# Two attention fills reordered: keys ahead of the norm, a projection that catches up inside the first groups, and later queries computed inside the second fill

## The chip, the cores and the metric

The kernel runs on one core of a Trainium2 chip. The metric is the time of one execution on the device in microseconds; the median of several runs is compared. Beside the timed runs one execution was recorded by the hardware profiler; its trace gives every instruction's start and duration on the five engines: TensorE (PE, with its weight loads as PEld), VectorE (DVE), ScalarE (ACT), GpSimd (POOL) and SyncE (SP, which here only issues transfers).

## The reference, cut to what matters

A residual stream `x` of 128 rows by 256 passes through six blocks; each starts with a norm of `x`. A context of 12544 rows by 192 is read by two of them. Only these two are touched.

```python
# block 1: 16 heads of 16, keys and values from the context
q = (layernorm(x) @ Wq + bq);  k = ctx @ Wk + bk;  v = ctx @ Wv + bv
out = softmax(q k^T / 4) v            # per head, over 12544 keys
x = x + relu(out @ W1 + b1) @ W2 + b2
# block 2: causal self-attention;  block 3: mixture of 8 experts
# block 4: 16 heads of 64, keys and values from the same context
q = layernorm(x) @ Wq;  k = ctx @ Wk;  v = ctx @ Wv
x = x + softmax(q k^T / 8) v @ Wo + bo
# block 5: small attention;  block 6: two of 8 experts
```

Everything is float32. The softmax subtracts a maximum over the keys, so the scores of many keys must exist before the first exponential.

## The kernel before, in words

**First attention.** The heads are done in two octets `j` (eight heads each). For each octet the context is walked in superblocks of 1024 keys (`SB`), numbered `m`; a superblock is four groups of 256 keys, numbered `t` over everything (98 groups). One group is one turn of the loop at L545. In a turn TensorE computes `scores(t)` (L412) into two score tiles, ScalarE copies both to SBUF (`keep`, L425) and VectorE keeps a running maximum (L431, or L437 for the first range, which reads the copies). Ten groups make a range; at its end the maxima are folded (`fold`), transposed and reduced (`range_maximum`), and spread over partitions (`range_spread`). `LAG` = 13 turns later the stored scores of a group are shifted by the maximum (GpSimd and VectorE, L493), exponentiated by ScalarE (L504) and multiplied with the values (`attend`, L517). So turns 0 to 11 are a fill: scores and projections only.

The projections of keys and values are cut into four pieces per superblock: `pieces(t)` gives for g = 0 the first half of the keys, g = 1 the second, g = 2 and 3 the same for values. A unit has a part with 64 contraction rows for both halves ("tiled", L214 or L232) and a part with 128 rows per half ("whole", L217 or L239). Its two PSUM banks come from the ring `ps_w`, of which there are two in this stage; a bank is free when it has been evicted (`keys_out` L373, `values_out` L377, both on VectorE). The pieces run `AHEAD` = 4 turns ahead: pieces 0 to 3 before the loop, then piece t + 4 in turn t. Other banks are tagged "m" (maximum) and "o" (output), one each; they are empty during the first turns.

Ahead of all this stand the loads of `x` and of small tensors, the norm `ln0` with its transposes, the broadcast of the value bias (`bvb`: a matmul of one row, L132, and a copy, L342), and the queries of both octets (L348 to L356).

**Between.** After the first attention a key projection for the second attention's pass 0 (`first_keys`, advanced in steps by `fill(n)`) is slipped between the steps of the following blocks.

**Second attention.** Eight passes `j` of two heads each walk 13 superblocks, one per period `t`; `LAG` is 14 periods. In pass 0 the keys are already there or come from `fill`; each period computes scores (L933), ScalarE copies them (L950), VectorE takes the maximum (L968). After the last period of the pass the maximum is folded (L980). All eight query chunks are computed before the first period (L876 and L880).

The order of the instructions on each engine is the order in which the program writes them (`manual_schedule`). SyncE issues all transfers in program order.

Of the kernel before, what the change touches and what calls it, by code (L numbers as in the profile page):

```python
# [33 lines left out]
def perceiver(ctx: ExitStack, tc: tile.TileContext, a: dict, out: bass.AP):  # L34
# [34 lines left out]

    x = xp.tile([P, D], F32, tag="x", name="x0")  # L70
    nc.sync.dma_start(x, a["x"][0])

# [54 lines left out]
    nc.sync.dma_start(cols, a["cols"])  # L127
    nc.sync.dma_start(rows, a["rows"])
# [6 lines left out]
    def layernorm(x, name):  # L135
# [10 lines left out]
        return xn, transposed(xp, xn, 2, name + "T", tag="xnT")  # L146

    def transposed(pool, t, n, name, tag, **kw):

        tT = pool.tile([P, n, P], F32, tag=tag, name=name, **kw)  # L150
        for g in range(0, n, 4):
            m = min(4, n - g)
            pt = ps_t(f"{name}_ps{g}")
            for i in range(m):
                nc.tensor.transpose(pt[:, i * P : (i + 1) * P], t[:, (g + i) * P : (g + i + 1) * P], ident)
            nc.vector.tensor_copy(tT[:, g : g + m, :].rearrange("p c n -> p (c n)"), pt[:, : m * P])
# [34 lines left out]
    def load_context(pool, name, s, bufs):  # L191
# [6 lines left out]
        nc.sync.dma_start(lo[:, :n], a["ctxT"][0:P, k0 : k0 + n])  # L198
        for r in range(2):
            nc.sync.dma_start(  # L200
# [4 lines left out]
    def project_keys(name, wk, cx, j):  # L205

        lo, hi, h = cx
        ps = [ps_w(f"{name}_{r}") for r in range(2)]
# [12 lines left out]
    def project_values(name, wv, cx, j):  # L221

        lo, hi, h = cx
        ps = [ps_w(f"{name}_{r}") for r in range(2)]
# [79 lines left out]
    with tc.tile_pool(name="l0w", bufs=1) as lw:  # L304
        xwq = slot_weight("xwq", a["L0_xattn_Wq"])
        xwk = context_weight(lw, "xwk", a["L0_xattn_Wk"])
        xwv = context_weight(lw, "xwv", a["L0_xattn_Wv"])

        with tc.tile_pool(name="l0x", bufs=1) as work, ExitStack() as ps0:
# [20 lines left out]
            for v in vs:  # L330
                nc.gpsimd.memset(v, 1.0)
# [6 lines left out]
            _, xnT = layernorm(x, "ln0")  # L338
            pb = ps_mm("bvb_ps")
            add_row(pb[:, :D], ROW_BV, D, start=True)  # L340
            bvb = work.tile([P, D], F32, name="bvb")
            nc.vector.tensor_copy(bvb, pb[:, :D])  # L342

            qz = work.tile([P, 2, 2, P], F32, name="x0_qz")
            for j in range(2):
                pq = ps_mm(f"x0_pq{j}")
# [10 lines left out]

            def pieces(t):
# [5 lines left out]
                if g == 0:  # L364
                    ctxs[m] = load_context(work, f"x0_ctx{m}", s, 2)
# [5 lines left out]

                def keys_out(r, src):
                    nc.vector.tensor_scalar(kTs[m][:, r * h : (r + 1) * h], src[:, :h], bias, None, ALU.add)  # L373

                def values_out(r, src):
                    n = h // P
                    nc.vector.tensor_copy(  # L377
                        v[:, r * n : (r + 1) * n, 0:136].rearrange("p k (h d) -> p k h d", d=17)[:, :, :, 0:16],
                        src[:, :h].rearrange("p (k h d) -> p k h d", h=8, d=16),
                    )  # L380

                def first_half(kind, make, w, evacuate):
                    unit = make(f"x0_{kind}{m}", w, ctxs[m], j)
# [66 lines left out]
            def bank_m(name):  # L450
                return pp.tile([P, KB], F32, tag="m", name=name, bufs=1)

# [53 lines left out]
            def attend(t):  # L506
                m, g = groups[t]
                b = range_of[t]
                if first[t]:
                    os[b] = pp.tile([P, KB], F32, tag="o", name=f"x0_o{b}", bufs=1)  # L510
# [27 lines left out]
            with tc.manual_schedule():  # L538
                for t in range(AHEAD):
                    for f in pieces(t):  # L540
                        f()
# [3 lines left out]
                for t in range(len(groups) + LAG + 1):  # L545
# [22 lines left out]
                    ahead = pieces(t + AHEAD)  # L568
# [14 lines left out]
                    if ended is not None:  # L583
                        range_maximum(ended)
                    if t > LAG and last[t - LAG - 1]:
# [4 lines left out]
            with tc.manual_schedule():  # L590
# [4 lines left out]

                kw = slot("k0_wk_lo"), slot("k0_wk_hi")
# [81 lines left out]
                nc.vector.tensor_tensor(o, om, bvb, ALU.add)  # L678
# [176 lines left out]
    with tc.tile_pool(name="l1x", bufs=1) as work:  # L855
# [10 lines left out]
        with tc.manual_schedule():  # L866
# [4 lines left out]
            for g in range(2):  # L871
                pq = ps_mm(f"x1_pq{g}")
                for i in range(4):
                    j = 4 * g + i
# [411 lines left out]
```

## Time and profile before

| | |
|---|---|
| runs | 1600.96, 1606.61, 1606.82 us; median 1606.61 |
| profiled execution | 1599.54 us, span 1597.8 us |
| mean granted TensorE clock | 0.988 |
| first attention's scores (L412) start | 22.11 us |
| first exponential (L504) | 72.48 us |
| end of the first attention's output matmuls (L517) | about 470 us |
| second attention's scores (L933) start | 594.30 us |
| its first fold (L980) | 634.98 us |

The times inside the span are from the span's start. In a timeline row the columns are start, duration, engine, line, operation, output and inputs, shape and the number of instructions merged into the row. In a row of stretches they are the stretch, its length, and the busy time of PE, PEld, DVE, ACT and POOL with the number of instructions, then the granted clock, the share of the DMA engines and GB/s. The chain of waits lists what the end of a window was waiting for, step by step; "issue" in it is time in which the engine waited for nothing that the profile shows.

### The profile page before, as it was taken

To read this page: it belongs to the slowest core of one execution; us is meant where nothing else is said; L and a number is where in the kernel's file an instruction comes from. 1 tells how busy PE (TensorE), PEld (TensorE's weight loads), DVE (VectorE), ACT (ScalarE), POOL (GpSimd) and SP (SyncE) were. 2 spreads that over 40 slices of the span, in tenths; PEclk is the share of its full clock that TensorE was granted. 3 is DMA by queue.
4 is the path that set the end of the run, shared out by engine and by line. 5 is a ranking of instruction groups with operands and counts; after the bars stand their busy time and mean duration, and the time that the engine had idled before them with its cause. 6 is when DMAs were issued, how large, how long until landed. Compare 5 with 4: busy or idle time off the path is not lost.

```text
span 1597.8 us, 39754 instructions
## 1 busy us (share of the span) xinstructions
PE 1511.6 (95%) x17130; PEld 1159.9 (73%) x17130; DVE 1181.8 (74%) x1254; ACT 986.4 (62%) x1205; POOL 857.1 (54%) x554
## 2 busy tenths in 40 slices
PE   7899999999879998999999999999999999998978
PEld 4566666666545886887777777787787778787868
DVE  5898987998883327678777777777777777777952
ACT  2699888999873226665665655665565655665631
POOL 1288888888840000863863864864764764762000
PEclk9999999999999999999999999999999999999979
DMA  3111021211096760232322222222232222225930
GB/s 103 41 49 54 27 61 41 61 41 41 14 255 180 241 169 20 80 99 68 96 83 83 82 80 86 80 84 81 84 97 79 86 80 85 81 80 160 297 135 4
DMA packets 68737, 146.62 MB, mean 92 GB/s; under 512 B 8905, under 2 KB 27089, under 8 KB 68562
## 3 DMA queue, kind: packets, MB, share of 16 engines
q1 hardware_dynamic: 68562, 144.08, 30.7%
q8 instruction: 135, 2.21, 0.6%
q14 instruction: 40, 0.33, 0.1%
HBM read 143.92 MB, written 0.13 MB: 90 GB/s over the span
## 4 chain that ended last, share of the span: by engine, by line
PE 74%; DVE 13%; ACT 7%; issue 3%; DMA 1%; POOL 1%; POOLq 0%; SPq 0%; ACTq 0%; DVEq 0%
PE x_v L239 12%; PE x_s L933 11%; PE x_k L217 11%; PE x_o L1018 10%; PE x_v L232 6%; PE x_k L214 5%; PE x_s L412 5%; DVE x_mx L431 4%; ACT x_p L425 3%; PE x_o L517 2%; PE f_h L1222 2%; PE f_h L801 2%; PE f_py L818 2%; DVE x_part L1041 2%; DVE x_p L493 2%
## 5 line engine op out<-in xcount | busy, mean ns | idle before, releaser
L999 POOL TENSOR_TENSOR x_p<-x_p,x_spread 128x1024 f32<-128x1024 f32 (+1 forms) x175 | 402.7, 2326 | 161.8 <-ACT x_spread L992 161.6
L493 POOL TENSOR_TENSOR x_p<-x_p,x_spread 128x512 f32<-128x512 f32 (+1 forms) x184 | 325.6, 1824 | 127.1 <-ACT x_spread L481 67.5
L1041 DVE TENSOR_REDUCE x_part<-x_p 128x256 f32<-128x1024 f32 (+1 forms) x175 | 329.7, 1924 | 1.6 <-ACT x_p L1007 1.6
L950 ACT COPY x_p<-x_s 128x1024 f32<-128x1024 f32 (+1 forms) x200 | 197.9, 996 | 179.8 <-DVE x_mx L957 97.9
L957 DVE TENSOR_TENSOR x_mx<-x_s,x_mx 128x1024 f32<-128x1024 f32 (+1 forms) x161 | 193.4, 1201 | 127.2 <-PE x_s L933 118.7
L1046 POOL TENSOR_TENSOR x_sums<-x_sums,x_part 128x256 f32<-128x256 f32 x161 | 120.9, 751 | 306.1 <-DVE x_part L1041 305.9
L425 ACT COPY x_p<-x_s 128x1024 f32<-128x1024 f32 x196 | 193.2, 1015 | 78.8 <-PE x_s L412 64.1
L239 PEld LDWEIGHTS x_v<-ywv_lo,x_ctx_lo 128*128 128x128 f32 x1568 | 192.3, 194 | 38.3 <-issue 36.8
L1007 ACT ACTIVATE x_p<-x_p 128x1024 f32<-128x1024 f32 (+1 forms) x200 | 197.8, 1037 | 1.4 <-DVE x_p L999 1.3
L504 ACT ACTIVATE x_p<-x_p 128x1024 f32<-128x1024 f32 x196 | 196.3, 1062 | 0.2 <-DVE x_p L493 0.2
L239 PE MATMUL x_v<-ywv_lo,x_ctx_lo 128*128 128x128 f32 x1568 | 196.2, 278 | 0.0
L1018 PE MATMUL x_o<-x_p,x_v 128*64 128x128 f32 x3136 | 193.8, 276 | 0.4
L431 DVE TENSOR_TENSOR x_mx<-x_s,x_mx 128x1024 f32<-128x1024 f32 x140 | 168.0, 1220 | 31.8 <-PE x_s L412 17.2
L1018 PEld LDWEIGHTS x_o<-x_p,x_v 128*64 128x64 f32 x3136 | 169.8, 137 | 12.4 <-issue 1.7
L933 PE MATMUL x_s<-x_qT,x_kT 64*128 64x128 f32 x2744 | 178.3, 279 | 0.0
L933 PEld LDWEIGHTS x_s<-x_qT,x_kT 64*128 64x128 f32 x2744 | 160.9, 188 | 15.8 <-issue 15.4
L217 PE MATMUL x_k<-x_ctx_lo,ywk_lo 128*128 128x512 f32 (+1 forms) x364 | 171.6, 594 | 0.0
L918 ACT COPY x_v<-x_v 128x512 f32<-128x512 f32 (+1 forms) x208 | 116.1, 562 | 83.3 <-PE x_v L239 82.8
L232 PEld LDWEIGHTS x_v<-ywv_hi,x_ctx_hi 64*128 64x128 f32 x1568 | 106.1, 188 | 47.2 <-issue 24.9
L412 PE MATMUL x_s<-x_qz,x_kT 32*128 32x256 f32 x1568 | 118.6, 401 | 17.0 <-ACT x_p L425 16.8
L517 PE MATMUL x_o<-x_p,x_v 128*32 128x128 f32 x3136 | 111.8, 276 | 9.8 <-ACT x_p L504 8.9
L517 PEld LDWEIGHTS x_o<-x_p,x_v 128*32 128x32 f32 x3136 | 82.0, 109 | 53.6 <-ACT x_p L504 19.8
(252 smaller groups left out, 1764.4 us busy)
## 6 DMA issues: line engine op xcount, KB each, us to landing
x_ctx_lo<-in_ctxT_dram SPq DMA_DIRECT2D x120, 512.0 KB, 4.1
x_ctx_hi<-in_ctxT_dram SPq DMA_DIRECT2D x240, 128.0 KB, 4.0
f_w<-in_L_ffn_W_dram SPq DMA_DIRECT2D x32, 512.0 KB, 4.9
k_lo<-in_ctxT_dram SPq DMA_DIRECT2D x12, 512.0 KB, 8.3
f_gating<-n_kernel_gating_EDF_dram SPq DMA_DIRECT2D x8, 512.0 KB, 6.8
f_up<-L_ffn_kernel_up_EDF_dram SPq DMA_DIRECT2D x8, 512.0 KB, 7.0
f_wd<-ffn_kernel_down_EFD_dram SPq DMA_DIRECT2D x8, 512.0 KB, 7.7
k_hi<-in_ctxT_dram SPq DMA_DIRECT2D x24, 128.0 KB, 8.3
```

The source lines that it names most:

```text
L217: nc.tensor.matmul(ps[r][:, :h], wk[0][:, js], lo[:, r * h : (r + 1) * h], start=False, stop=True)
L232: nc.tensor.matmul(ps[r][:, ks], hi[rs, ks], wv[1][rs, js], start=(kc == 0), stop=False, skip_group_check=True,)
L239: nc.tensor.matmul(ps[r][:, kc * P : (kc + 1) * P], lo[:, r * h + kc * P : r * h + (kc + 1) * P], wv[0][:, js], start=False, stop=True, sk ...
L412: nc.tensor.matmul(st[i // 2][:, i % 2, 256 * c : 256 * c + 256], kTs[m][rs, ks], qz[rs, sbs[m][0]].rearrange("p u q -> p (u q)"), start=T ...
L425: nc.scalar.copy(ps[t][k], st[k].rearrange("p a n -> p (a n)"))
L431: nc.vector.tensor_tensor(m, st[1 - k], old, ALU.max)
L493: engine.tensor_tensor(v, v, by[:, banks].unsqueeze(2).to_broadcast([P, n, 2, 256]), ALU.add)
L517: nc.tensor.matmul(os[b][32 * i : 32 * i + 32, u * P : (u + 1) * P], v[:, 2 * g + c, 17 * (2 * i + u) : 17 * (2 * i + u) + 32], p[i // 2][ ...
L933: nc.tensor.matmul(st[:, u, c * P : (c + 1) * P], kTs[t][rs, ks], qT[rs, j, :], start=True, stop=True)
L999: engine.tensor_tensor(v, v, spreads[j].unsqueeze(2).to_broadcast([P, 2, n, P]), ALU.add)
L1018: nc.tensor.matmul(o[us, 0:P], vs[t][:, c0 + c, us], p[:, n0 : n0 + P], start=(c0 + c == 0), stop=(c0 + c == total - 1), skip_group_check= ...
L1041: nc.vector.tensor_reduce(part, v, AX.X, ALU.add)
```

## The change

In the first attention, the first superblock's context is loaded through ScalarE's queue, and the key weights move ahead of the columns and query weights on SyncE's. The first half of the first key projection comes before the norm on TensorE; the norm's transposes and the queries of octet 0 use the two halves of one score tile (`early`). Then the loop starts. Pieces 1 to 7 are done in turns 0 to 3, two per turn and one in turn 3 (`behind`); from turn 4 on it is piece t + 4 as before. The values of the first two superblocks go to the banks "m" and "o" (`spare`). Pieces below 16 (`filling`) are evicted by ScalarE, keys as an Identity activation with the bias. The queries of octet 1 come in turn 5. The value tiles are set to one only where a one is needed. The bias row's matmul moves behind the loop, and its bank is read directly by the addition; the load of `rows` moves to turn 8.

In the second attention, only query chunk 0 comes ahead of the first period; chunks 1 to 4 come in period 5 and chunks 5 to 7 in period 7, each group followed by one scaling on VectorE.

```diff
-    nc.sync.dma_start(cols, a["cols"])
-    nc.sync.dma_start(rows, a["rows"])
...
     with tc.tile_pool(name="l0w", bufs=1) as lw:
+        x = xp.tile([P, D], F32, tag="x", name="x0")
+        nc.sync.dma_start(x, a["x"][0])
+        xwk = context_weight(lw, "xwk", a["L0_xattn_Wk"])
+        nc.sync.dma_start(cols, a["cols"])
         xwq = slot_weight("xwq", a["L0_xattn_Wq"])
-        xwk = context_weight(lw, "xwk", a["L0_xattn_Wk"])
         xwv = context_weight(lw, "xwv", a["L0_xattn_Wv"])
...
-                nc.gpsimd.memset(v, 1.0)
+                nc.gpsimd.memset(v[:, :, 0:136].rearrange("p k (h d) -> p k h d", d=17)[:, :, :, 16:17], 1.0)
+                nc.gpsimd.memset(v[:, :, 136:152], 1.0)
...
+            def spare(name):
+                return bank_o(name) if name.endswith("_1") else bank_m(name)
+            def behind(t):
+                return ((1, 2), (3, 4), (5, 6), (7,))[t] if t < 4 else (t + AHEAD,)
...
-                    ctxs[m] = load_context(work, f"x0_ctx{m}", s, 2)
+                    ctxs[m] = load_context(work, f"x0_ctx{m}", s, 2, None if m else nc.scalar)
...
+                filling = t < LAG - 1 + AHEAD
                 def keys_out(r, src):
-                    nc.vector.tensor_scalar(kTs[m][:, r * h : (r + 1) * h], src[:, :h], bias, None, ALU.add)
+                    dst = kTs[m][:, r * h : (r + 1) * h]
+                    if filling:
+                        nc.scalar.activation(dst, src[:, :h], AF.Identity, bias=bias)
+                    else:
+                        nc.vector.tensor_scalar(dst, src[:, :h], bias, None, ALU.add)
                 def values_out(r, src):
...
+                    evacuated(filling, dst, src[:, :h].rearrange("p (k h d) -> p k h d", h=8, d=16))
                 def first_half(kind, make, w, evacuate):
-                    unit = make(f"x0_{kind}{m}", w, ctxs[m], j)
+                    bank = spare if kind == "v" and m < 2 else None
+                    unit = make(f"x0_{kind}{m}", w, ctxs[m], j, bank)
...
             with tc.manual_schedule():
-                for t in range(AHEAD):
-                    for f in pieces(t):
-                        f()
+                tiled, whole, k_out = pieces(0)
+                tiled()
+                whole()
+                early = ps_s("x0_early")
+                _, xnT = layernorm(x, "ln0", early[:, 0])
+                k_out()
+                queries(0, xnT, early[:, 1])
...
-                    ahead = pieces(t + AHEAD)
+                    ahead = [f for n in behind(t) for f in pieces(n)]
...
+                    if t == 5:
+                        queries(1, xnT, bank_m("x0_pq1"))
+                    elif t == 8:
+                        nc.sync.dma_start(rows, a["rows"])
...
+                pb = ps_mm("bvb_ps")
+                add_row(pb[:, :D], ROW_BV, D, start=True)
...
-                nc.vector.tensor_tensor(o, om, bvb, ALU.add)
+                nc.vector.tensor_tensor(o, om, pb[:, :D], ALU.add)
...
-            for g in range(2):
-                pq = ps_mm(f"x1_pq{g}")
-                for i in range(4):
-                    j = 4 * g + i
+            def queries(j0, j1):
+                pq = ps_mm(f"x1_pq{j0}")
+                for j in range(j0, j1):
...
+            queries(0, 1)
...
                 if t < NS:
                     fill(2 if t < 4 else 1)
+                if t in (5, 7):
+                    queries(*((1, 5) if t == 5 else (5, 8)))
```

## The prediction

> **What bounds the kernel now.** I read four views in this order: the busy shares, the busy time by stretch, the chain of waits in the first 80 us, and the timeline of the two places where the change cuts in.
>
> ```profile
> PE 1511.6 (95%) x17130; PEld 1159.9 (73%) x17130; DVE 1181.8 (74%) x1254; ACT 986.4 (62%) x1205; POOL 857.1 (54%) x554
> ```
>
> TensorE is busy 95% of the span, so a gain must come from a stretch where it stands idle or starts late. The stretches (length; then busy us of PE, PEld, DVE, ACT, POOL):
>
> ```profile
> 0.00:5.00 5.00, 0.00 (x0) 0.00 (x0) 0.72 (x4) 1.37 (x2) 4.37 (x24) 1.00 0.39 122
> 40.00:50.00 10.00, 9.14 (x85) 6.09 (x86) 7.14 (x9) 5.08 (x6) 0.00 (x0) 1.00 0.01 2
> 80.00:100.00 20.00, 19.22 (x314) 13.49 (x316) 17.64 (x21) 18.66 (x21) 20.00 (x12) 1.00 0.14 41
> ```
>
> At 80 us all engines overlap; at 40 us GpSimd has nothing to do and ScalarE is half idle: that is the fill, in which scores are stored until the first range's maximum is known. Before it, TensorE does nothing for 8 us. The start, and the chain inside the fill:
>
> ```profile
> 5.44 2.45 DVE L145 TENSOR_SCALAR ln<-x,ln_mv,ln_rstd 128x256 f32<-128x256 f32 x1
> 11.78 2.71 PE L214 MATMUL x_k<-x_ctx_hi,xwk_hi 64*128 64x512 f32 x4
> 14.42 3.78 PE L217 MATMUL x_k<-x_ctx_lo,xwk_lo 128*128 128x512 f32 x4
> 22.11 1.15 PE L412 MATMUL x_s<-x_qz,x_kT 32*128 32x256 f32 x16
> ```
> ```profile
> 43.49 0.14 DVE x_mx L437
> 43.63 0.99 issue
> 44.63 0.75 DVE x_kT L373
> 45.38 0.04 issue
> 45.42 1.16 PE x_v L232 x14
> ```
>
> The reader is to see two things. First, norm, bias row, queries, keys and values run one after another, so the first scores start at 22.11. Second, inside the fill TensorE's next projection waits for a bank that VectorE empties (L373), and VectorE gets to it only after the maxima (L437). Score groups start at 25.30, 40.12 and 54.95 for t = 1, 5, 9: 14.8 us for four groups.
>
> The second fill is another case:
>
> ```profile
> 589.11 5.26 PE L876 MATMUL x_pq<-ln3T,ywq 128*128 128x128 f32 x32
> 612.98 21.96 DVE L968 TENSOR_TENSOR x_mx<-x_p,x_mx 128x1024 f32<-128x1024 f32 x17 [0.98 <-ACT x_p L950]
> 634.98 1.89 DVE L980 TENSOR_REDUCE x_folded<-x_mx 128x256 f32<-128x1024 f32 x1
> ```
>
> All eight query chunks precede the first score (594.30), but the stage ends with the maxima: from 612.98 VectorE runs 17 of them without a hole, and the fold follows. Its queue bounds this fill, not TensorE's.
>
> **The change part by part.** Sums are against the profiled execution: 1599.5 us, span 1597.8, so 1.7 us around it. The median shown, 1606.6, is 7.1 us above it (the runs go from 1601.0 to 1606.8); I carry the difference over to the median.
>
> *Start of TensorE.* The first context block goes to ScalarE's queue at about 0.85 us instead of SP's at 6.06. In the trace its large part landed 5.8 us after issue and its small parts 4.3. By the row it would be here at about 6.3 to 6.7. The Trainium skill, "DMA: Bandwidth & Descriptors", section "Issuing engines are not separate DMA queues", speaks against a larger gain: transfers from any engine run on the same 16 engines and a second issuer saves only issue time. Up to here 1.19 MB must come in (x 128 KB, key weights 256, columns 38, context 768), against some 340 GB/s in the trace at 8 to 9.7 us: 3.5 us and about 2 us of latency, so 6.3 by that way too. x may land later than its 2.9; its norm has until 10.8. On SP's queue the query weights now wait for the context's landing (they share a completion counter) and come at about 9.5; needed at 11.9. The value weights follow at about 10 (needed at 17.8) and the second block at about 14 (needed at 23): covered, else a delay goes straight into TensorE. The columns, now behind the key weights on SP, come at about 5 and are first read at 10.9. ScalarE spends some 1.6 us on its three issues (0.5 each on SP) before its table load, which started at 3.62 in the trace: covered as well.
>
> From 6.3: key halves 2.71 (as at 11.78), one whole-key matmul 1.9 (half of 3.78), to 10.9. Two transposes 0.66, VectorE copy 0.42 with semaphores 0.1, queries of octet 0 four records 1.05, then 0.35 + 0.48 on VectorE and 0.15 of semaphores: first scores at 14.1, 8.0 us earlier. The norm (2.45 while GpSimd clears the value tiles, 0.41 for the other five in the trace) is off the path: smaller memsets are worth nothing here, but had it stayed slow it would still fit.
>
> *Catching up.* Eight groups' pieces stood ahead of, or inside, t = 0 to 3 before; now k's first half is done early and pieces 1 to 7 lie inside t = 0 to 3. TensorE pays in order: scores 1.09, k tiled 1.06, each whole half 1.07, v tiled 1.08. While the clock is low, times 1.7 (3.78 us for four L217 records at 14.4 us, 2.2 later). Here a rule and the row part. "TensorE: Matmul & The Clock Gate", section "What's actually happening", gives full clock after about 3.4 us of sustained work; in this trace matmuls start at 8.04 and the L217 records to 18.2 are still slow: 10 us. By the rule the array would be fast by 11 and the fill 2 to 3 us shorter; I take the row, slow until about 18.5.
> t0: 1.85 + 1.8 + 1.85 + 1.07, so t1 at 20.7; t1: 1.09 + 1.07 + 1.06 + 1.07 = 4.3, t2 at 25.0; likewise t3 at 29.3; t3: 2.2, t4 at about 31.4 against 35.0. Lead 3.6: more than half of the start's 8 us is given back.
>
> *Evacuation by ScalarE for t < 16.* Sixteen evictions leave VectorE (0.75 and 0.69 us). The nearest ScalarE row of this shape is L632, 0.585 us; with bias or a strided destination I take 0.6 (ends 0.4 and 1.0). Behind each wait the next group's score copies. Four groups then need: TensorE 11.1 (4.4 scores, 3.2 k, 3.3 v and 0.2), ScalarE 8 x 0.97 + 4 x 0.6 = 10.1, VectorE 8 x 1.2 = 9.6. With the holds between (a score tile cannot be overwritten before its copy of 0.97 ends) I get 12.1 per four groups against 14.8: t8 at 43.6 against 49.84, t10 at 49.5 against 57.19. Between t10 and t11, VectorE does maxima, fold and two reductions without the key and value evictions that stood between them (6.74 us before): about 5.3. t11 at 54.8 against 63.93, t12 at 58.0 to 58.4 against 67.55: 9.2 us. An eviction of 1.0 us instead of 0.6 would cost 1.3 of it. The later query pair (0.83 us on VectorE, 0.8 on TensorE at t = 5) falls into VectorE's slack, included. The instruction order has activation-table loads only where before (square root and exponential), so none is added. From t = 12 the order is the same, and the 9.2 us are carried to its end at 470.
>
> *The bias row.* Its matmul (0.69 for two records at this clock) now precedes the key fill at 471.38. The transposes of the result waited there for TensorE (end 477.3, data 477.0), so +0.65. The addition reads PSUM instead of SBUF, 0.42 either way. The late load of the rows, 5 KB, is hidden by hundreds of us.
>
> *Second fill.* Before the first score go 4 records instead of 32: 28 x 0.162 = 4.5 us less, but VectorE's 0.35 is now waited for: scores at 590.3, 4.0 earlier. VectorE would do its maxima 4.0 earlier too, until t = 5. There the maxima of t4 end at 611.6; the queued scaling waits for the sixteen records behind the scores of t5: 609.0 + 1.99 + 0.42 + 16 x 0.13 (L686, the same shape, sixteen records in 2.05) + 0.2 = 613.7. So 2.1 idle and 0.69 of scaling; at t7 0.2 and 0.55. Given back: 3.6. Net -0.4; at the 0.162 of L876 it would be +0.3, so I keep -2 and +1.5 as ends. What is moved is work into the cover of a queue that is itself the bound.
>
> Sum: -9.2 + 0.65 - 0.4 = -9.0. 1599.5 would become 1590.5; the median 1597.6.
>
> **The rivals.**
> *Early clock* (12%): the rule on the clock holds in the new order, since dense work begins at 6.3. Then -12 us, 1594.6. For it: no idle of over a microsecond in the keys. Against: 10 us in the trace.
> *The catch-up is held* (14%): ScalarE's eviction, queued behind two score copies, keeps a bank; or a context block comes late. One hold of 1 us in each of four groups: -5, 1601.6. Against: values of the first two blocks get two otherwise empty banks.
> *The slow clock stays* (4%): two waits for the norm at about 11.4 and 13 break TensorE's work. Each four groups at 1.7 times lose 5 to 7 us. By the same recurrence the first part's gain is gone if the clock stays low to about 43 us, and over 8 us are lost if it lasts to 60. Against: by 18.2 it rose in the trace despite gaps of 0.6 us. That is the one way to a slower kernel.
> *It doesn't do what it says*: true of the second part, where I count 0.4 us; counted in the main case.
>
> **How the numbers follow.** Main case 70%, -7 to -11 us. Half a percent (8.0 us) is about what a measurement of this kernel tells from no change, and the estimate lies only 1 us beyond it: of the 70, 50 fall above and 20 below. Early clock adds 12 to faster; the held catch-up 14 to same. Slow clock: 3 slower, 1 same. Faster 0.62, same 0.35, slower 0.03. Range: a gain of 12 on the lowest run shown (1601.0) gives 1589; a gain of 3.5 on 1606.8 gives 1603.3.
>
> **What would show it.** First scores near 14 us with keys from about 6.3; t4 near 31, t12 near 58; ScalarE rows of about 0.6 us for keys and values; no VectorE eviction between the maxima. In the second fill: scores at 4 us less after the norm, a hole of about 2 us in VectorE before the scaling of t5, and a fold as far after the norm as before. The prediction is wrong if t12 gains under 6 or over 12 us, or if the second fill moves by over 2.

## The result and the profile after

The changed kernel takes 1593.86 us (median of 5, 1592.18 to 1594.52), the kernel before 1600.96 us (median of 5 beside it, 1599.76 to 1606.82). The ratio is 0.9947, with a 95% interval of 0.9925 to 0.9969: faster by 7 us in the medians, and by 6.9 us between the two profiled executions (1592.66 us against 1599.54; spans 1590.9 and 1597.8). The prediction said 1597.6 (1589.0 to 1603.3), 9.0 us less. Its 1597.6 was counted from 1606.61, the median of three runs; counted from the 1600.96 of the five runs beside the change, the same forecast is 1592.0. The forecast of the whole is right; one of its steps is not, and most of this part is about that.

Busy shares of the changed kernel, and its row of the clock in 40 slices:

```profile
PE 1507.9 (95%) x17130; PEld 1156.8 (73%) x17130; DVE 1169.4 (74%) x1238; ACT 996.3 (63%) x1221; POOL 851.1 (54%) x559
...
PEclk9999999999997999999999999999999999999979
```

VectorE has lost 16 instructions and ScalarE has got them. The clock row has a 7 in slice 13 (477 to 517 us), where the kernel before has a 9; the change touches nothing there. The stretches that the prediction showed (busy us of PE, PEld, DVE, ACT, POOL; clock; DMA share; GB/s):

```profile
0.00:5.00 5.00, 0.00 (x0) 0.00 (x0) 0.60 (x4) 0.00 (x0) 3.12 (x31) 1.00 0.64 198
40.00:50.00 10.00, 9.52 (x76) 4.80 (x72) 7.40 (x7) 7.97 (x11) 0.00 (x0) 1.00 0.27 79
```

The first 5 us move 1.6 times the bytes (198 GB/s against 122), and in the fill ScalarE is busy 7.97 of 10 us, where it was 5.08. TensorE's timeline at the start, and the groups of ScalarE's evictions between 13 and 44 us (busy us, mean ns):

```profile
6.59 2.55 PE L209 MATMUL x_k<-x_ctx_hi,xwk_hi 64*128 64x512 f32 x4 [6.59 <-DMA xwk_hi<-in_L_xattn_Wk_dram]
...
12.09 0.71 PE L344 MATMUL x_early<-ln0T,xwq 128*128 128x128 f32 x4 [0.52 <-DVE ln0T L150]
13.86 1.15 PE L428 MATMUL x_s<-x_qz,x_kT 32*128 32x256 f32 x16 [1.05 <-DVE x_qz L352]
...
18.17 1.15 PE L428 MATMUL x_s<-x_qz,x_kT 32*128 32x256 f32 x16
```
```profile
L254 ACT COPY x_v<-x_v 128x512 f32<-128x512 f32 x6 | 3.6, 596 | 2.1 <-PE x_v L234 2.1
L388 ACT ACTIVATE x_kT<-x_k,cols 128x512 f32<-128x512 f32 x5 | 3.5, 697 | 1.4 <-PE x_k L212 1.4
```

First scores come at 13.86 us instead of 22.11. A values' eviction on ScalarE takes 0.596 us, a keys' eviction, which adds a bias, 0.697. The second fill on VectorE:

```profile
611.91 0.69 DVE L903 TENSOR_SCALAR x_qT<-x_pq 128x512 f32<-128x512 f32 x1 [1.78 <-PE x_pq L899]
...
617.84 0.56 DVE L903 TENSOR_SCALAR x_qT<-x_pq 128x384 f32<-128x384 f32 x1
...
632.32 1.88 DVE L1005 TENSOR_REDUCE x_folded<-x_mx 128x256 f32<-128x1024 f32 x1
```

The hole ahead of the first scaling is there, 1.78 us (2.1 was predicted), and the second scaling has none.

Where the time went, both profiled executions side by side (start of the event, us):

| event | before | changed | difference |
|---|---|---|---|
| first scores | 22.11 | 13.86 | -8.25 |
| first exponential | 72.48 | 62.11 | -10.37 |
| last attend product of the first attention | 468.96 | 458.92 | -10.04 |
| transposes of its output | 477.30 | 469.47 | -7.83 |
| first query product of the self-attention | 488.93 | 481.09 | -7.84 |
| output product of the self-attention | 518.24 | 517.09 | -1.15 |
| last addition of the experts | 585.32 | 584.18 | -1.14 |
| fold of the second fill | 634.98 | 632.32 | -2.66 |
| first attend product of the second attention | 650.03 | 644.67 | -5.36 |
| end of span | 1597.8 | 1590.9 | -6.9 |

10.4 us are won in the fill and 2.5 lost again up to 481 us, most of it at the bias row. Another 6.7 are lost between 481 and 517 us in a stage that the change leaves alone, and 5.8 are won behind it, where the prediction expected 0.4. The granted clock says how. Stretches of 490 to 520 us, before and changed (the number behind the five engines is the clock):

```profile
490.00:500.00 10.00, 7.79 (x49) 5.88 (x48) 7.20 (x8) 4.00 (x10) 0.00 (x0) 1.00 1.02 306
500.00:510.00 10.00, 8.85 (x22) 3.91 (x22) 1.98 (x4) 4.96 (x14) 0.00 (x0) 0.66 0.18 61
510.00:520.00 10.00, 10.00 (x57) 6.64 (x58) 3.06 (x8) 1.75 (x3) 0.00 (x0) 1.00 0.36 106
```
```profile
490.00:500.00 10.00, 7.50 (x16) 3.34 (x14) 3.23 (x5) 6.95 (x20) 0.00 (x0) 0.66 0.06 6
500.00:510.00 10.00, 9.84 (x43) 7.54 (x42) 2.60 (x5) 0.59 (x1) 0.00 (x0) 0.66 0.27 99
510.00:520.00 10.00, 10.00 (x26) 4.69 (x28) 2.44 (x7) 1.34 (x3) 0.00 (x0) 0.66 0.16 54
```

A mean of 0.66 is 6.8 us at half clock and 3.2 at full: in stretches of a quarter of a microsecond, the clock is either 1.00 or 0.50. In the kernel before it is halved from 499.97 to 506.80; in the changed one from 462.25 to 465.67, from 492.98 to 499.81 and from 503.21 to 516.87. The distances between these six edges are 3.42, 27.31, 6.83, 3.40 and 13.66 us: whole steps of 3.41 us. The same grid runs through the whole execution (the changed kernel is at half clock from 1527.21 to 1544.28, five steps). Its phase, that is where its edges lie when they are taken modulo 3.413 us, is another in each: 0.48 of a step in the profile before, 0.43 after. Both profiles have one wait of TensorE of 2.5 us in this stage; the rest of the lost stretch is not waiting, for TensorE is busy 9.84 and 10.00 of 10 us. From 510 to 520 us it has 26 product records, where the kernel before has 57. From here on such a step at half clock is called a slow window.

### The profile page after: what moved, and what is told of

It is laid out like the page before. It is cut to its first block, busy times and chain, and to the rows that moved or that the text cites. A ratio compares the mean times of both kernels' runs of the same rounds, so it can differ in the third digit from the quotient of the medians.

```text
span 1590.9 us, 39751 instructions
## 1 busy us (share of the span) xinstructions
PE 1507.9 (95%) x17130; PEld 1156.8 (73%) x17130; DVE 1169.4 (74%) x1238; ACT 996.3 (63%) x1221; POOL 851.1 (54%) x559
## 4 chain that ended last, share of the span: by engine, by line
PE 62%; DVE 6%; ACT 2%; POOL 1%; DMA 1%; issue 1%; SPq 0%; DVEq 0%; ACTq 0%
PE x_s L958 11%; PE x_v L234 10%; PE x_o L1043 10%; PE x_k L212 9%; PE x_v L227 5%; PE x_k L209 4%; PE f_h L1249 2%; PE f_h L824 2%; PE k L212 2%; PE f_py L841 2%; DVE x_part L1066 1%; POOL x_p L506 1%; PE k L209 1%; DVE x_folded L1005 1%; PE f_py L1258 1%
## 5 line engine op out<-in xcount | busy, mean ns | idle before, releaser
L1043 PEld LDWEIGHTS x_o<-x_p,x_v 128*64 128x64 f32 x3136 | 169.6, 137 | 12.3 <-issue 1.5
```

The lines of the kernel that those rows point to most:

```text
L1043: nc.tensor.matmul(o[us, 0:P], vs[t][:, c0 + c, us], p[:, n0 : n0 + P], start=(c0 + c == 0), stop=(c0 + c == total - 1), skip_group_check= ...
```

## The experiments

Each kernel is the changed one (or the one before, where said) with a short edit. Ratios are to the kernel before on the same chip (three chips, on which its medians are 1600.2 to 1601.2 us); its 71 executions beside the experiments have a median of 1601.1 us.

**The two parts alone.** `first_only` is the changed kernel with the second attention's fill as before; `second_only` is the kernel before with this and no more:

```diff
-            for g in range(2):
-                pq = ps_mm(f"x1_pq{g}")
-                for i in range(4):
...
+            queries(0, 1)
...
                     fill(2 if t < 4 else 1)
+                if t in (5, 7):
+                    queries(*((1, 5) if t == 5 else (5, 8)))
```

(These are the lines that `second_only` adds and `first_only` takes back.)

> The changed first attention with the second attention's fill as it was before. Theory 'clock windows': the 10.4 us that the first attention gains are there (first exponential near 62.1 us), and some 7 us of them are lost again between the first query product of the self-attention (481.1) and the end of the experts (584.2), because TensorE's granted clock is halved there in whole steps of 3.41 us (17 us of slow clock against 6.8 before), so the experts end near 584.2 here too, and the whole is 1 to 4 us shorter than the kernel before: 1596 to 1600 us. Rival 'the second part is worth nothing': this kernel is as fast as the full change, 1594 us. Rival 'the weights of the experts arrive when they did': the experts end at 584 to 585 too, but with the clock full.

> The kernel before with only the second attention's queries changed (pass 0 ahead, passes 1 to 4 in period 5, 5 to 7 in period 7). By the prediction's own step: first scores of the fill 4.0 us earlier, fold 0.4 us earlier, -0.4 us in all (-2 to +1.5). Theory 'clock windows': the two slow windows at 636.5 to 643.3 us go as well, since TensorE no longer idles some 4 us ahead of the fold's end: -4 to -6 us, 1595 to 1597 us. Rival 'the fill is bound by VectorE alone': -1.5 us at the fold and no more afterwards.

`first_only`: 1595.41 us, ratio 0.9959 (0.9945 to 0.9973). `second_only`: 1600.77 us, 0.9999 (0.9987 to 1.0011). The first part is the whole gain within what is measured, and the second is worth nothing within some 2 us: the expectation of -4 to -6 us for it was wrong. The expected end of the experts in `first_only` (584.2) was wrong too, in a telling way: 579.44, with the grid at phase 0.66 and 3.4 us of slow clock in the self-attention instead of 20.5. The rival 'the weights of the experts arrive when they did' falls as well: from the output product of the self-attention to the last addition of the experts it takes 67.08 or 67.09 us in each of the 14 profiles, without a wait of TensorE, so the experts end as much earlier as they begin.

**Is TensorE's idle stretch the cause?** At 490.5 us TensorE of the changed kernel stands still for 2.50 us:

```profile
492.97 2.03 PE L209 MATMUL k<-k_hi,k_wk_hi 64*128 64x512 f32 x2 [2.50 <-issue]
```

The profile names no releaser. The next PSUM bank still holds the self-attention's values, which VectorE copies out behind masks and maxima; its copy ends at 492.87. `after_v` and `before_v` move that copy ahead of the scores, into a hole of VectorE:

```diff
+            nc.vector.tensor_copy(v[:, :, 0:16], pv[:, :D].rearrange("p (h d) -> p h d", d=16))
             acc = work.tile([P, NH, 17], F32, name="a0_acc")
...
-            nc.vector.tensor_copy(v[:, :, 0:16], pv[:, :D].rearrange("p (h d) -> p h d", d=16))
             fill(3)
```

> The changed kernel with one copy moved: the self-attention's values leave their PSUM bank ahead of the scores on VectorE's queue, where VectorE has been idle for 2.7 us, and not behind the masks and maxima of both groups of heads; TensorE then need not wait 2.5 us (490.5 to 493.0) for that bank. Theory 'clock windows': without that idle stretch the clock stays full from 490 to 517 us (20.5 us of slow clock now), the experts end 7 to 10 us earlier (574 to 577), and the whole takes 1583 to 1587 us. Rival 'the weights of the experts arrive when they did': the self-attention ends up to 2.5 us earlier, the experts end at 583 to 584 as now, and the whole takes 1593 to 1594 us.

> The kernel before with the same copy moved ahead of the scores. Theory 'clock windows': the 2.5 us of idle TensorE at 498.3 and the two slow windows behind it (499.97 to 506.80) go: 2.5 us and about half of 6.8 us, so 4 to 6 us shorter, 1595 to 1597 us. Rival 'the weights arrive when they did': 0 to 1 us, 1600 to 1601 us.

`after_v`: 1597.24 us, 0.9975 (0.9964 to 0.9986). `before_v`: 1602.64 us, 1.0000 (0.9986 to 1.0014). Neither is faster for it, and the slow windows in the stage are 17.1 us in `after_v` and 20.5 us in `before_v` (6.8 in the kernel before). The theory was not tested by these two, for the wait had only moved. TensorE and ScalarE of `after_v`:

```profile
492.56 1.13 PE L209 MATMUL k<-k_hi,k_wk_hi 64*128 64x512 f32 x4
...
498.75 1.14 PE L149 MATMUL a_pT_ps<-ident,a_p 128*128 128x128 f32 x8 [3.14 <-ACT k L655]
```
```profile
493.40 4.83 ACT L774 ACTIVATE a_p<-a_sm,a_nmax 128x128 f32<-128x128 f32 x16 [5.04 <-DVE a_nmax L771]
498.13 2.01 ACT L655 COPY k<-k 128x512 f32<-128x512 f32 x4
```

The next bank is held by four copies of keys that stand behind 16 exponentials on ScalarE's queue; TensorE stands 3.14 us, now right ahead of the narrow products with the values.

**The banks freed as well.** `after_vk` adds to `after_v` that one pair of those key copies goes ahead of the exponentials and the next pair to VectorE; `after_again` is the changed kernel unaltered.

```diff
             load_pair(6)
             fill(1)
+            flush()
...
             fill(3)
+            flush(nc.vector.tensor_copy)
             load_pair(8)
```

(`flush` issues the two copies of the last finished key tile, on ScalarE unless told otherwise.)

> The changed kernel with the values' copy ahead of the scores as in after_v, and with the evictions of two key tiles of the second attention moved: one pair ahead of the 16 exponentials on ScalarE's queue, the next pair to VectorE behind the maxima, so that no PSUM bank is held behind the exponentials (in after_v TensorE waited 3.14 us for such a bank at 495.6). Theory 'idle TensorE brings the slow windows': no wait of TensorE above 1 us between 485 and 515 us, so at most one or two slow windows there (3 to 7 us, against 17 in after_v and 20.5 in the changed kernel); from the first query product to the output projection 26 to 29 us (34.1 in after_v, 36.0 in the changed kernel), the whole 5 to 8 us below the changed kernel: 1586 to 1589 us. Rival 'the narrow products (17 columns) bring the slow windows, idle or not': 10 us or more of slow clock stay, 31 us or more for that stretch, the whole 2 to 4 us below.

> The changed kernel once more, unaltered. Theory 'clock windows with a phase of their own': the edges of the granted clock lie on a grid of 3.41 us within the run, at another phase than the 0.43 of a step seen so far; first exponential between 62.1 and 65.5 us according to that phase (with the phase, the first window in which the clock is full comes up to 3.4 us later), the slow windows between 460 and 520 us differ in number from the 7 seen (20.5 us + 3.4 us), and the time lies between 1590 and 1598 us. Rival 'the slow windows belong to the code': the same windows within 0.5 us, and 1592 to 1594.5 us.

`after_vk`: 1589.07 us, 0.9924 (0.9905 to 0.9943). `after_again`: 1593.98 us, 0.9956 (0.9942 to 0.9971). TensorE of `after_vk` and its stretches:

```profile
498.96 1.04 PE L149 MATMUL a_pT_ps<-ident,a_p 128*128 128x128 f32 x8
499.92 1.71 PE L209 MATMUL k<-k_hi,k_wk_hi 64*128 64x512 f32 x4
501.57 1.96 PE L790 MATMUL a_av<-a_v,a_pT 128*128 128x17 f32 x16
```
```profile
490.00:500.00 10.00, 9.82 (x59) 7.06 (x59) 7.30 (x9) 4.74 (x13) 0.00 (x0) 1.00 0.23 72
500.00:510.00 10.00, 10.00 (x56) 6.35 (x56) 4.64 (x10) 2.92 (x8) 0.00 (x0) 1.00 0.35 108
510.00:520.00 10.00, 10.00 (x46) 5.44 (x45) 3.27 (x14) 5.39 (x8) 0.00 (x0) 1.00 0.63 208
```

No wait above 0.81 us, no slow window, and the narrow products (17 columns) run at full clock: the rival that blames these alone falls. From the first query product to the output product it takes 22.80 us. The same length in all 14 profiles, ordered by where the grid lies (the share of a step from the first query product to the next edge of the grid):

| share of a step | slow clock in the stage, us | length, us (kernel) |
|---|---|---|
| stage as it was: | | |
| 0.05, 0.07 | 6.8, in two pieces | 29.45 (`q_act`), 29.43 (`bias_in_loop`) |
| 0.21, 0.23 | 6.8 | 29.28 (`second_only`), 29.31 (before) |
| 0.41 | 6.8 | 29.55 (`after_again`) |
| 0.48 | 20.5 | 36.00 (changed) |
| 0.75, 0.79, 0.81 | 3.4 | 28.04 (`q_later`), 28.09 (`first_only`), 28.08 (`warm`) |
| 0.99 | 17.1 | 34.34 (`no_act`) |
| values' copy moved: | | |
| 0.18 | 20.5 | 35.14 (`before_v`) |
| 0.79 | 17.1 | 34.13 (`after_v`) |
| banks freed as well: | | |
| 0.04, 0.38 | 0 | 22.80 (`all_in`), 22.80 (`after_vk`) |

Where the grid lies alike, an unaltered stage has the same slow windows and the same length to 0.05 us, whether the kernel has the change or not. At equal phase one also sees what the edits do: moving only the copy makes it worse (`after_v` against `first_only`, `before_v` against `second_only`), and freeing the banks takes the slow windows away (`all_in` against `q_act`, `after_vk` against `after_again`). Within the unaltered stage each microsecond of slow clock costs (36.00 - 28.07) / 17.1 = 0.46 us; of the 5.3 us between 22.80 and 28.07, 2.5 are the wait, 1.1 the products that it drives apart (two pairs of key products take 1.12 and 1.09 us around it, all four 1.13 without it), and 1.7 the slow window (3.68 us for the next four, against 1.98). The changed kernel's profile has 20.5 us, its repetition 6.8: the 6.7 us that the first table shows as lost belong to that execution's phase, not to the change. `after_again` differs in the same way at the start:

```profile
7.09 2.49 PE L209 MATMUL x_k<-x_ctx_hi,xwk_hi 64*128 64x512 f32 x4 [7.09 <-DMA xwk_hi<-in_L_xattn_Wk_dram]
...
12.53 1.22 PE L344 MATMUL x_early<-ln0T,xwq 128*128 128x128 f32 x4 [0.52 <-DVE ln0T L150]
14.80 2.09 PE L428 MATMUL x_s<-x_qz,x_kT 32*128 32x256 f32 x16 [1.05 <-DVE x_qz L352]
```

The queries that took 0.71 us in the first profile take 1.22, the scores 2.09 instead of 1.15. The first record of the clock, the moment at which it is first granted in full, stands at 19.56 us in this trace, at 11.70 in the first profile. Group 1 follows at 21.34 instead of 18.17, the first exponential at 65.28 instead of 62.11.

**ScalarE's evictions.** `no_act` leaves the evictions of the fill to VectorE:

```diff
-                filling = t < LAG - 1 + AHEAD
+                filling = False
```

> The changed kernel with the keys and values of the fill evicted by VectorE as before, in place of ScalarE (the catch-up order stays). By the prediction's step (12.1 us for four groups with ScalarE, 14.8 with VectorE; 12.74 measured): a period of 14.3 to 14.8 us again, scores of group 12 some 3 to 5 us later counted from those of group 0 (43.3 us in the changed kernel, 46.5 to 48.5 here), the whole 3 to 5 us above the changed kernel. Rival 'the fill is bound by TensorE or by the transfers': within 1 us.

1595.62 us, 0.9959 (0.9944 to 0.9975). Scores of groups 4 and 8 start at 29.29 and 43.10: 13.81 us for the four groups (12.74 in the changed kernel; 14.8 expected). From group 5 to 9, behind the catch-up, it is 14.83, as expected. Group 12 comes 46.60 us after group 0, against 43.33 in the changed kernel, whose groups 0 and 1 also lie 4.31 us apart. So the step is worth 3.3 us at group 12 (and the first exponential comes at 65.67 instead of 62.11). The end does not show it: the ratio is that of the changed kernel within its interval. The slow windows of the single executions can move the whole by more than the step is worth.

**The queries' scaling.** `q_act` scales the later passes on ScalarE; `q_later` leaves them on VectorE, one period after their products:

```diff
+                q = qT[:, j0:j1, :].rearrange("p j n -> p (j n)")
+                if j0:
+                    nc.scalar.activation(q, pq[:, : (j1 - j0) * P], AF.Copy, scale=0.125)
+                else:
+                    nc.vector.tensor_scalar(q, pq[:, :P], 0.125, None, ALU.mult)
```
```diff
+                if t in (6, 8):
+                    scaled(*later)
                 if t in (5, 7):
-                    queries(*((1, 5) if t == 5 else (5, 8)))
+                    later = queries(*((1, 5) if t == 5 else (5, 8)))
```

> The changed kernel with the later query passes of the second attention scaled on ScalarE (periods 5 and 7) in place of VectorE. Prediction's step 'what is won at the start is given back on VectorE': VectorE's hole of 1.78 us and its 0.69 and 0.56 us go, and the fold begins 2.5 to 3.5 us earlier counted from the norm's transpose (632.32 - 586.85 = 45.5 us in the changed kernel, 42.0 to 43.0 here); the whole 1.5 to 3.5 us below the changed kernel. Rival 'the fill is bound by the scores' PSUM banks and ScalarE's copies': ScalarE then waits for the queries in VectorE's place, and the fold is less than 1 us earlier; the whole within 1 us of the changed kernel.

> The changed kernel with the scaling of the later query passes (0.69 us and 0.56 us on VectorE) one period after their matmuls (periods 6 and 8 instead of 5 and 7), so that VectorE does not wait for TensorE. Theory 'VectorE's queue is held for queries that no one needs yet': the hole of 1.78 us ahead of the first scaling goes, and the fold begins 1.0 to 1.8 us earlier counted from the norm's transpose (45.5 us in the changed kernel without a slow window in that stage, 46.8 with one), so 43.7 to 44.5 us (1.4 more with a slow window); the whole 1 to 2 us below the changed kernel. Rival (after q_act) 'the hole is TensorE's, which does 1.95 us of query products between scores, and comes back as a wait for the scores': less than 0.5 us.

`q_act`: 1596.75 us, 0.9973 (0.9962 to 0.9984). From the copy of the norm's transpose to the fold 49.60 us with one slow window, where `after_v` and `after_again` with one take 46.84: 2.8 us worse, and the expectation was wrong. ScalarE now waits for the queries, holds its score copies, TensorE waits for their banks and VectorE for their maxima:

```profile
609.73 0.60 ACT L905 ACTIVATE x_qT<-x_pq 128x512 f32<-128x512 f32 x1 [3.52 <-PE x_pq L899]
611.26 5.21 DVE L995 TENSOR_TENSOR x_mx<-x_p,x_mx 128x1024 f32<-128x1024 f32 x4 [3.38 <-ACT x_p L977]
611.29 2.08 PE L960 MATMUL x_s<-x_qT,k 64*128 64x128 f32 x32 [1.65 <-ACT x_p L977]
```

`q_later`: 1594.61 us, 0.9949 (0.9930 to 0.9967); 47.43 us with two slow windows against 48.41 to 48.47 for four kernels with two and the scaling as in the change. The 1.0 us is at the lower end of what was expected: the hole of 1.78 us went, and waits of 0.67 and 0.24 us for score copies came back. The whole does not tell it from the changed kernel.

**The bias row.** `bias_in_loop` puts its product and copy into turn 10 of the loop:

```diff
+                    elif t == 10:
+                        pb = bank_m("bvb_ps")
+                        add_row(pb[:, :D], ROW_BV, D, start=True)
+                        bvb = work.tile([P, D], F32, name="bvb")
+                        nc.vector.tensor_copy(bvb, pb[:, :D])
...
-                pb = ps_mm("bvb_ps")
-                add_row(pb[:, :D], ROW_BV, D, start=True)
```

> The changed kernel with the bias row's product and copy in turn 10 of the first attention's loop in place of behind it. By the prediction's step (0.65 us) and what the changed kernel showed (0.69 us, and a slow window behind it): counted from the last attend product (458.92 in the changed kernel) to the transposes of the output (469.47, 10.55 us; 8.34 us in the kernel before), 9.9 us if only the 0.69 us go, 8.3 to 8.6 us if the slow window goes with it; the whole 0.7 to 2.2 us below. Rival 'the slow window comes of the narrow products ahead, the bias row has nothing to do with it': the slow window stays in this run if the grid falls alike, 9.9 us.

1594.62 us, 0.9950 (0.9932 to 0.9968). TensorE behind the loop, in the changed kernel and here:

```profile
461.34 0.69 PE L126 MATMUL bvb_ps<-rows,ones 1*128 1x256 f32 x2 [0.39 <-DMA cpw<-in_L_attn_c_proj_w_dram]
461.97 1.83 PE L209 MATMUL k<-k_hi,k_wk_hi 64*128 64x512 f32 x4
```
```profile
468.00 1.20 PE L209 MATMUL k<-k_hi,k_wk_hi 64*128 64x512 f32 x4 [0.39 <-DVE x_accs L546]
```

From the last attend product to the output's transposes it takes 8.35 us, as in the kernel before (8.34), and 10.55 in the changed kernel. `q_act` has the bias row but no slow window there, and its transposes come 7.31 us after those of the last range (465.05 to 472.36; 6.75 in `bias_in_loop`, 8.96 in the changed kernel): the row itself costs 0.56 us, a slow window 1.65 more. One begins within 461 to 469 us in six of the nine profiles with the bias row behind the loop, in none of the five without. By the grid (share of a step from the last range's transposes to the next edge): at 0.34 to 0.46 the three profiles with the row there have the window (`after_vk`, `after_again`, the changed kernel), the two without it have none (`all_in`, `bias_in_loop`); at 0.49 to 0.57 none of five has it, with the row or without. So at some phases the row brings the window. The phase is not all, for at 0.25 and 0.26 two profiles with the row differ (`warm` has it, `q_later` not). Nor is the row free in the loop: group 12 comes 4.04 us behind group 11 with it, 3.62 without, and the whole does not tell `bias_in_loop` from the changed kernel.

**Keeping TensorE busy.** `warm` fills idle stretches with products of ones by ones into a bank that no one reads: 20 ahead of the first keys, 12, 20 and 12 around the last self-attention (in which the written order now also is the order of all engines).

```diff
             with tc.manual_schedule():
+                warm(ps_s("x0_warm")[:, 0], 20)
                 tiled, whole, k_out = pieces(0)
...
-    with tc.tile_pool(name="l1a", bufs=1) as work:
+    with tc.tile_pool(name="l1a", bufs=1) as work, tc.manual_schedule():
+        warm(ps_mm("a1_warm0"), 12)
...
+        warm(ps_mm("a1_warm1"), 20)
         nmax = small.tile([P, 1], F32, tag="s_nmax", name="a1_nmax")
...
+        warm(ps_mm("a1_warm2"), 12)
         x = residual(x, pa[:, :D], "x5a")
```

> The changed kernel with products of ones by ones into a bank that no one reads, where TensorE idles: 20 of 128 columns ahead of the first keys, and 12, 20 and 12 in three holes of the last self-attention; nothing of the computation changes. Theory 'the clock follows how busy TensorE has been': the first key products run at full clock (0.28 us each instead of 0.64), the first scores come at 11.5 to 12.5 us (13.86 and 14.80 seen), those of group 1 at 15.5 to 17 us (18.17 and 21.34 seen); the five slow windows of the tail (1527 to 1544 us, 17.07 us in every run so far) shrink to two or fewer, worth 2 to 4 us there; the whole 4 to 8 us below the changed kernel. Rival 'the clock follows the program's time or power, not activity': the same slow stretches, and the whole 0 to 3 us above for the products that delay others.

1589.96 us, 0.9923 (0.9904 to 0.9942). The clock is granted in full from 4.03 us. First scores at 12.53, group 1 at 16.84, first exponential at 60.78 us, 1.3 earlier than in the first profile of the change and 4.5 earlier than in `after_again`. The five slow windows of the last self-attention, which the twelve profiles without these products all have (17.07 us, in one piece or two), are one (3.4 us). So the clock follows what TensorE does, and not the program's time. In the tail the products and the fixed order came together and were not tried apart; at the start the order was fixed before.

**All of it.** `all_in` has the edits of `after_vk`, `q_later`, `bias_in_loop` and `warm`.

> The changed kernel with all of it: values' copy and key evictions moved as in after_vk, bias row in the loop, queries scaled a period later, and the products of ones. If the gains add up: after_vk's 5 us, 4 to 8 us of the warm clock, 1 to 2 us of the scaling and 1 to 2 us of the bias row: 1579 to 1584 us. If the windows of the clock only fall elsewhere: 1587 to 1590 us, as after_vk.

1577.59 us (1577.01 to 1580.65), 0.9856 (0.9831 to 0.9882): 22.6 us below the kernel before, better than the sum expected. It has six slow windows in all (20.5 us), where the changed kernel's profile has twelve (41.0 us). Its last self-attention and the first expert behind it, with the first expert of the changed kernel below:

```profile
1517.56 4.63 PE L123 MATMUL a_warm<-ones 128*128 128x128 f32 x40
1522.41 0.30 PE L153 MATMUL a_spT_ps<-ident,a_spn 128*128 128x128 f32 x1 [0.21 <-DVE a_spn L1233]
...
1528.09 2.03 PE L1270 MATMUL f_h<-ln5T,f_gating 128*128 128x128 f32 x16
```
```profile
1534.01 0.45 PE L149 MATMUL a_spT_ps<-ident,a_spn 128*128 128x128 f32 x1 [4.27 <-DVE a_spn L1213]
...
1540.95 3.62 PE L1249 MATMUL f_h<-ln5T,f_gating 128*128 128x128 f32 x16
```

Two records are one product here. At the start 20 products were too many in this execution: they ran to 8.8 us, the first keys waited, and a slow window came at 14.13; its first exponential is at 63.72.

## Why the prediction was right, and which step was not

*Start.* Keys from 6.38 to 7.63 us in the nine profiles with this start (6.3 predicted); in the two shown they were released by the key weights and not by the context. x landed at 4.36 us instead of 2.89, inside the slack that was named. The norm took 0.41 us, off the path. First scores at 13.86 to 15.77 (14.1).

*The clock.* Here the prediction weighed a row (slow until about 18.5) against the rule of the Trainium skill, "TensorE: Matmul & The Clock Gate", section "What's actually happening" (full clock after some 3.4 us of activity, in windows that run freely), and took the row. In the changed kernel's profile the rule's number came: full clock from 11.70, the end of the first whole step of the grid after TensorE began at 6.59. In `after_again` the row's came, 19.56. Groups 0 and 1 lie 4.31 us apart in the changed kernel and `no_act`, 6.3 to 7.2 in the seven other profiles with this start (6.6 predicted). The grid divides them: in these two its next edge lies 0.50 of a step behind the first keys, and full clock comes 5.1 us after these; in the seven it lies elsewhere (0.05 to 0.25, 0.60 to 0.65 and 0.98), and full clock comes 12.3 to 14.5 us after. So "slow until 18.5" and "early clock" are not two theories: both are outcomes of one kernel, and the second, given 12%, was seen twice in nine. Putting a single execution's clock into the sum as if it belonged to the code is the step that failed; that it hit the commoner outcome was luck.

Nor is it settled what brings full clock. Every earlier step of `after_again` had a hole of half a microsecond or more in it, but holes are not the whole reason. In the kernel before TensorE's products leave no gap from 8.04 to 18.87 us, and full clock comes at 18.69, after three whole busy steps; the gaps of 0.6 us that the prediction speaks of are not in the products' rows. `after_vk` has a step without a gap (7.48 to 10.89) and stays slow to 21.13. In `warm` a step 83% busy with products of ones was enough. One busy step of 3.4 us, as the page has it, is thus not always enough here; which products count was not tested.

*Catching up and evictions.* Four groups take 12.74 us (12.1): a keys' eviction takes 0.697 us, not 0.6, a values' eviction 0.596. Group 10 to 11 takes 5.5 us (5.3). Group 12 is at 57.19 in the early outcome, 60.41 in `first_only` and 60.35 in `after_again` (58.0 to 58.4), against 67.55. Over all profiles of each start, without those that edit it, the first exponential is at 73.64 us on average before (3 profiles) and 65.07 after (7): 8.6 us less, where 9.2 less was predicted. The gain at group 12 is 10.4 us in the first pair of profiles and 7.1 to 7.2 in `first_only` and `after_again`, inside the 6 to 12 that the prediction set.

*Bias row.* 0.56 us of its own (0.65), and 1.65 more where a slow window follows.

*Second fill.* First scores came earlier and the scaling gave it back, as said. From the copy of the norm's transpose to the fold, at equal slow clock: 45.39 us with all queries ahead (`before_v`) and 45.47 with the change, without a slow window; 46.99 (before, `first_only`) and 46.84 (`after_v`, `after_again`) with one. That is -0.15 to +0.1; predicted was -0.4 (-2 to +1.5). The 1.5 us in the first table are a slow window that the profile before had at 588.72 and the one after had not. The 2.7 us behind the fold are two more: from fold to first attend product every profile takes 12.4 us without, 13.7 to 14.0 with one, 14.9 to 15.1 with two.

*The sum.* -8.6 and +0.6 to 2.2 and nothing for the second part is -6 to -8; measured -7. The prediction's -9.0 is too much mainly by the slower catch-up (12.74 us for four groups, with the keys' eviction at 0.697) and the window at the bias row. The rival "early clock" named 1594.6, close to the measured 1593.86, but by the way of the higher median of the three runs: its gain of 12 us was not there. That no step of the sum lay between 481 and 650 us was right on average, though the two profiles differ there by +6.7 and -4.2 us. The last 1.5 us of the first table are one more slow window, at 1459 us, which only the profile before has.

## What to carry over

Before explaining a difference between two profiles, compare the granted clock stage by stage: here a stage that no edit touched differed by up to 8 us (28.04 to 36.00), as much as the whole change was worth, and its length agreed to 0.05 us between profiles whose grid lay alike. A wait removed in front of a stretch can only move to the next held bank: follow every bank to the queue that empties it, and move evictions ahead of long work on that queue. Idle TensorE cost more than its own length here, so where its waits can't be removed, it is worth filling them with work of no use, as long as this ends before the data come.

## What the runs showed of the hardware

The granted clock changes only on a grid of 3.41 us, at another phase in each execution (14 profiles: 0.14 to 0.84 of a step); the rule named above says as much of the window, and the trace's edges agree. In the rows the clock reads 1.00 from the first moment, though the first products run at half speed: the record begins only where the clock is first granted in full (11.70 us in the changed kernel's trace), so the start has to be read from the products' own durations. And no stage is safe: nine of the 14 profiles have slow windows at the end of the first attention's steady part too (420 to 445 us), and `before_v` and `second_only` have one in the first fill (at 30 and 45 us). What it costs can be read from the clock of whole executions: of the kernel before, the 11 executions with a mean clock of 0.983 or less average 1606.3 us, the 19 with 0.988 or more 1599.3. So most of this kernel's scatter between executions goes with the clock.

How much idle time within a window brings the next one down is not settled. With the 2.5 us of it in the unaltered self-attention there were 3.4 to 20.5 us of slow clock behind, according to the phase; in the changed kernel the window from 499.81 to 503.21 had only 0.16 us of it between records, and four slow ones followed. In `after_v` and `before_v`, where the idle stretch of 3.1 us lay next to the narrow products, it was 17.1 and 20.5 us; without an idle stretch none in two profiles. That narrow products and idle time add up would fit, but was not measured apart.
